# Two causal attention layers: heads in two 64-row strips, the triangle zeroed after the exponential, the key mask as a contraction row

## The chip, the cores and the metric

The kernel runs on one core of a Trainium2 chip. The metric is device time in microseconds (us), here the median of three runs. An instruction's line (L460 is line 460 of the kernel before) names where it is written; matmuls of the attention layers all go through one helper, so they carry L460 (matmul) or L463 (transpose) and are told apart by their tiles.

The engines: PE multiplies matrices (PEld are its weight loads), DVE is the vector engine, ACT the scalar engine, POOL is GpSimd, and SP is the sync engine, which here only issues DMAs. A "q" behind a name (SPq, ACTq) is that engine's sequencer, where DMA issues are shown.

## The reference

A pre-norm decoder with four blocks of self-attention, cross-attention and a feed-forward layer: 8 batches, 256 positions, 128 channels, 512 context positions, all float32. Only two of the twelve layers are changed, both in the last block. Both are causal with 16 heads of 8 channels:

```python
# L3_attn
scores = jnp.einsum('bhid,bhjd->bhij', Qh, Kh) / jnp.sqrt(jnp.asarray(Dh, dtype=x.dtype))
causal = jnp.tril(jnp.ones((S, S), dtype=x.dtype))
scores = scores * causal - NEG_BIG * (1.0 - causal)
attn = jax.nn.softmax(scores, axis=-1)
# L3_xattn: keys from the context
scores = jnp.where(mask[:, None, None, :] == 0, neg_inf, scores)
future = jnp.triu(jnp.ones((Sq, Sk), dtype=bool), k=1)
scores = jnp.where(future[None, None, :, :], neg_inf, scores)
attn = jnp.nan_to_num(jax.nn.softmax(scores, axis=-1), nan=0.0)
```

In L3_xattn the triangle hides every key past 255, so only the first 256 context positions take part. Its output is multiplied by a sigmoid gate of the queries before the output projection.

## The kernel before

`_heads_attention` (L478) computes five attention layers with many heads, the two causal ones with `causal=True`. Everything stays in SBUF. One **step** of its loop (the `while t < end` near L690) is one head of one batch: 16 heads times 8 batches make 128 steps, with a software pipeline:

- `maxima(t)`: the scores of head t with queries on the partitions, in two matmuls (`mh_sps`, 128x128 and 128x256, because the upper right quarter is not needed). DVE takes the row maxima off them in one custom reduce each (L523), which also adds the causal mask (a bf16 tile, `causal`; in L3_xattn a tile `km_q` that holds the key mask too).
- `turn`, every four heads: POOL splits the negated maxima into a rounded part and a rest (`mh_hi`, `mh_nx`; L549, L551, L552).
- `turned`, two steps later: PE transposes them (`mh_mps`, L463), ACT copies them to `mh_m` (L561), and a DMA on ACT's queue (L563) writes them into rows 96 and 97 of the query tile `mh_q`, so that the next matmul subtracts them.
- `exps(t-12)`: the scores again, keys on the partitions (`mh_bsps`): first a bf16 matmul that writes the mask (the identity times the triangle, 256 columns, in L3_attn; `km_k` times the identity, 384 columns, in L3_xattn), then two matmuls of 256 and 128 columns onto it. ACT takes the exponential (L583, `mh_e`).
- `combine`, every four heads, 16 steps behind `maxima`: 16 matmuls `mh_ops` that multiply by the values; four heads sit on four 32-column strips of the array. Then copies (`mh_osb`, L629), transposes (`mh_otps`), the division, and once per batch the output projection (`mh_yps`), the residual and the next layer's normalization.

While batch b runs, `hd.steps(b + 1)` prepares the next one: at head 2 the keys are projected (`mh_kps`, biased on ACT at L426, split in two parts on POOL at L428 and L429 into `mh_kp`), at head 3 the queries (`mh_qps`), and at heads 5 to 10 SP's queue spreads them over partitions: 4 DMAs of 16x8x256 for keys (L434) and 8 of 8x8x256 for queries (L439) into `mh_k` and `mh_q`. A head's 8 channels, in hi and lo parts, take 32 rows; even heads lie in rows 0 to 31 and odd ones in 32 to 63 of a 96-row contraction with zeros between. There are two key tiles of two halves, two query tiles, and a third query tile that `third()` (L377) sets up with four ACT copies and, for the key mask, the transposed triangle `causal_t` on POOL, between the layers at 1284 us.

The key mask is prepared by `_l3_masks` (L792) at step 72 of L3_attn: a 1 MB load that repeats the mask on all partitions, four DVE operations (L804), and then `key_bias`, for each batch two `km_q` (L813, L814) and two `km_k` operations on POOL (L816, L817).

PE's order is that of the program. The order on the other engines is set by the scheduler of the language, among what each pool's buffers allow: `mh_sps` and `mh_ops` share three PSUM buffers, `mh_bsps` has three, everything else two (`hd_g`). While L3_attn starts, the last normalizations of the layer before run as a "guest", at the pace given; the normalization of the following layer's input is part of this loop.

Of the kernel before, what the change touches and what calls it, by code (L numbers as in the profile page):

```python
# [40 lines left out]
P = 128  # L41
# [5 lines left out]
TOP = 96  # L47
FLOOR = -1.0e20
# [118 lines left out]
def _pack(inputs):  # L167
# [3 lines left out]
    for layer, mats in w.items():  # L171
# [8 lines left out]
    arrays["key_mask"] = np.ascontiguousarray(np.asarray(inputs["mask_BxS2_ik0"])[:, :S]).reshape(1, B * S)  # L180
    arrays["key_mask_t"] = np.ascontiguousarray(
        np.asarray(inputs["mask_BxS2_ik0"])[:, :S].reshape(B, 2, P).transpose(2, 0, 1)
    ).reshape(P, 2 * B)
# [161 lines left out]
class _Heads:  # L345
# [5 lines left out]
    def __init__(self, E, ctx):  # L351
# [10 lines left out]
        self.made = 0  # L362
# [14 lines left out]
    def third(self, ctx):  # L377

        pool = ctx.enter_context(self.E.tc.tile_pool(name="hd3", bufs=1, side="right"))
        q = pool.tile([P, H, S], F32R, name="mh_q2")  # L380
        for i in range(0, H, 4):
            self.E.nc.scalar.copy(
                q[:, i : i + 4, :].rearrange("p h n -> p (h n)"), self.E.plain[:, 0:1].to_broadcast([P, 4 * S])
            )
        self.q.insert(0, q)

        t = self.E.causal_t = pool.tile([P, 3, P], F32, name="causal_t")
        self.E.nc.gpsimd.memset(t, 0.0)
        for i in (0, 2):
            self.E.nc.gpsimd.affine_select(  # L390
                out=t[:, i, :], in_=t[:, i, :], compare_op=ALU.is_ge, fill=NEG, base=0,
                pattern=[[1, P]], channel_multiplier=-1,
            )

    def begin(self, layer, keys, bias=True):

        E, nc, W = self.E, self.E.nc, self.E.w(layer)
        self.layer, self.keys, self.bias = layer, keys, bias
        self.n = keys(0).shape[1]
        self.ready = {}  # L400
        if bias:

            ps = self.g.tile([P, D], F32, tag="g", name="mh_bps")
            bvt = self.one.tile([P, D], F32, tag="bvt", name="mh_bvt")
            nc.gpsimd.tensor_copy(bvt, W("bv").to_broadcast([P, D]))
            nc.tensor.matmul(ps, bvt, W("wo"), start=True, stop=True)
            self.row = self.one.tile([P, D], F32, tag="row", name="mh_row")
            nc.vector.tensor_tensor(self.row, ps, W("bo"), ALU.add)

    def steps(self, b):  # L410
# [29 lines left out]

        def values():
# [11 lines left out]
        two = lambda f, g: lambda: (f(), g())  # L453
        spread = [lambda j=j: spread_k(j) for j in range(4)]
        spread += [lambda r=r, j=j: spread_q(r, j) for j in range(4) for r in range(2)]
        early = [lambda: project("k", self.keys(b), n), lambda: project("q", E.xt(b), S), rest]
        return early, [two(*spread[i : i + 2]) for i in range(0, 12, 2)], values
# [20 lines left out]
def _heads_attention(E, ctx, causal=False, mask=None, key_bias=None, gate=False, guest=None, known=(0,), pace=None):  # L478
# [10 lines left out]
    lag = 12 if causal else 8  # L489
# [4 lines left out]
    pe = pool("mhe", 8 if causal else 10)  # L494
# [13 lines left out]
    units, extras = {}, {}  # L508

    def maxima(t):  # L510

        b, h = divmod(t, H)
        if h == 0 and key_bias:
            extras[b] = key_bias(b)
        if h % 4 == 0:
            u = units[t // 4] = SimpleNamespace(r=ready[b], es={}, extra=extras.get(b))
            u.nm = sm.tile([P, 2, 4], F32, name="mh_nm")
        u = units[t // 4]
        q, k = u.r.q[:TOP, h, :], u.r.k[:TOP, h // 2, :]
        def lowest(at, scores, lowered):  # L520

            rest = wk.tile([P, S if causal else n], BF16, name="mh_rest")
            nc.vector.tensor_tensor_reduce(  # L523
                rest[:, : scores.shape[1]], scores, lowered, -1.0, -FLOOR, ALU.add, ALU.min, accum_out=at
            )

        col = slice(h % 4, h % 4 + 1)
        if causal:
            ps = ps_a.tile([P, 3 * P], F32, tag="a", name="mh_sps")
            mm(ps[:, :P], q[:, :P], k[:, :P], start=True, stop=True, skip_group_check=True)  # L530
            mm(ps[:, P:], q[:, P:], k, start=True, stop=True, skip_group_check=True)
            by = (u.extra or E.causal)[0].rearrange("p i k -> p (i k)")
            lowest(u.nm[:, 0, col], ps[:, :P], by[:, :P])
            lowest(u.nm[:, 1, col], ps[:, P:], by[:, P:])
            return
        for c in range(2):
            ps = ps_a.tile([P, n], F32, tag="a", name="mh_sps")
            mm(ps, q[:, c * P : c * P + P], k, start=True, stop=True, skip_group_check=True)
# [5 lines left out]
    def turn(i):  # L544

        u = units[i]
        nm = u.nm
        hi = sm.tile([P, 2, 4], F32R, name="mh_hi")
        nc.gpsimd.tensor_copy(hi, nm)  # L549
        u.nx = sm.tile([P, 2, 2, 4], F32, name="mh_nx")  # L550
        nc.gpsimd.tensor_copy(u.nx[:, :, 0, :], hi)  # L551
        nc.gpsimd.tensor_tensor(u.nx[:, :, 1, :], nm, hi, ALU.subtract)  # L552

    def turned(i):
# [3 lines left out]
        for c in range(2):  # L558
            turn_over(ps[:8, c, :], u.nx[:, c, :, :].rearrange("p a h -> p (a h)"))
        m = wk.tile([8, S], F32R, name="mh_m")  # L560
        nc.scalar.copy(m, ps[:8].rearrange("p c q -> p (c q)"))  # L561
        h0 = 4 * (i % 4)
        nc.scalar.dma_start(u.r.q[TOP : TOP + 2, h0 : h0 + 4, :].bitcast(F32), m.bitcast(F32))  # L563

    def exps(t):

        u, h = units[t // 4], t % H
        if causal:
            ps = ps_b.tile([P, 384], F32, tag="b", name="mh_bsps")
            if u.extra:  # L570
                mm(ps, E.ident16, u.extra[1], start=True, stop=False, skip_group_check=True)
            else:
                mm(
                    ps.rearrange("p (i q) -> p i q", q=P)[:, 0:3:2, :], E.later,
                    E.ident16.unsqueeze(1).to_broadcast([P, 2, P]), start=True, stop=False, skip_group_check=True,
                )
            for kt in range(2):
                mm(
                    ps[:, 256 * kt : 256 + P * kt], u.r.k[:, h // 2, kt * P : kt * P + P],
                    u.r.q[:, h, kt * P :], start=False, stop=kt == 1, skip_group_check=True,  # L580
                )
            e = pe.tile([P, 384], F32, tag="e", name="mh_e")
            nc.scalar.activation(e, ps, AF.Exp, scale=scale)  # L583
            u.es[h % 4, 0], u.es[h % 4, 1] = e[:, :S], e[:, S:]
# [48 lines left out]
    def divide(b, s2):  # L633
# [8 lines left out]
        if key_bias is not None:  # L642
# [34 lines left out]

    normed_already = set(range(B) if guest is None else known)
# [10 lines left out]
    free = lag + 4  # L689
    t, end = 0, H * B + lag + 4  # L690
    while t < end or todo:
# [18 lines left out]
        if t < H * B:  # L710
            maxima(t)
            if t % 4 == 3:
                turn(t // 4)
        if guest:
            visit(pace(t))
        if t % 4 == 1 and 4 < t < H * B + 2:
            turned(t // 4 - 1)
        if 0 <= t - lag < H * B:
            exps(t - lag)
        c = t - lag - 4  # L720
# [71 lines left out]
def _l3_masks(E, ctx):  # L792
# [3 lines left out]
    mk = ctx.enter_context(E.tc.tile_pool(name="kmb", bufs=2))  # L796
    kb = pool.tile([P, B, 2, P], BF16, name="km")
    kt = pool.tile([P, B, 2], F32, name="km_t")
    with E.tc.tile_pool(name="km_raw", bufs=1) as rp:
        raw = rp.tile([P, B * S], I32, name="km_raw")  # L800
        nc.sync.dma_start(raw, E.ins["key_mask"].to_broadcast([P, B * S]))
        flat = kb.rearrange("p b i k -> p (b i k)")
        for i in range(0, B * S, 512):
            nc.vector.tensor_scalar(flat[:, i : i + 512], raw[:, i : i + 512], 0.0, NEG, ALU.is_equal, ALU.mult)  # L804
        rt = rp.tile([P, B * 2], I32, name="km_rt")
        nc.sync.dma_start(rt, E.ins["key_mask_t"])
# [975 lines left out]
```

## Time and profile before

| what | us |
| --- | --- |
| median of 3 runs (lowest, highest) | 1773.42 (1773.2, 1773.54) |
| span of the profiled execution | 1770.2 |
| L3_attn, first key projection to that of the next layer | 1325.7 to 1527.8 |
| L3_xattn, first key projection to its end | 1527.8 to 1707 |
| PE busy in the whole span | 1462.7 (83%) |
| DVE, ACT, POOL busy | 1148.5, 881.5, 495.7 |

The profiled execution's own time is not listed beside these runs; its span is 3.2 us below the median. Busy time is the time in which an engine has at least one instruction running, and matmuls overlap, so a busy PE can still be given more work; where PE's cost is at stake, the distance from one start to the next is read. A row of the timeline view gives the start, the duration, engine, line, operation, output and inputs, the number of instructions and, in brackets, how long the engine had been idle and what released it. The row of a DMA issue gives the time that the issuing engine spends on it, not the transfer's. A figure in the PEclk column is the clock that the throttle granted to PE, as a share of full speed.

### The profile page before, as it was taken

The page shows a single profiled execution, that of the slowest core. Times are in us where ns is not written, and L with a number is a line of the kernel's source. Part 1 is how long each engine was busy: PE and PEld are TensorE (multiplying, and loading weights), DVE is VectorE, ACT ScalarE, POOL GpSimd, SP SyncE. Part 2 cuts the span into 40 slices and gives each one's busy share as a digit, 9 for nine tenths or more (in the row PEclk, how much of TensorE's full clock was granted, in tenths as well). Part 3 has the DMA queues.
Part 4 walks back from the last instruction along what each step waited for, and adds up shares of the span by engine and source line. Part 5 has one row for each costly group of instructions (what it writes and reads, how often), then busy time and mean ns, then how long its engine had stood idle before and what let it go on. Part 6 is the DMA issues. An engine that isn't in the chain of part 4 may idle for free. (4 is left out here: it accounts for less than half of the span.)

```text
span 1770.2 us, 29308 instructions
## 1 busy us (share of the span) xinstructions
PE 1462.7 (83%) x10103; PEld 1055.3 (60%) x10141; DVE 1148.5 (65%) x3857; ACT 881.5 (50%) x1830; POOL 495.7 (28%) x987
## 2 busy tenths in 40 slices
PE   5689989999999998785578888878946799799986
PEld 3457677766665555453446666656615677677763
DVE  4567666765636676777667777767465666466756
ACT  7245455555652344325535655557644466355543
POOL 3122222221110122223433433332113433244422
PEclk9799999999999999997979999989956899899998
DMA  4011011104100000000111101111002221122100
GB/s 154 13 37 36 6 34 37 36 11 155 38 1 1 1 1 1 0 1 1 36 35 36 28 14 37 37 37 45 2 10 65 85 69 38 50 55 59 39 1 25
DMA packets 47236, 60.43 MB, mean 34 GB/s; under 512 B 5232, under 2 KB 36976, under 8 KB 46448
## 3 DMA queue, kind: packets, MB, share of 16 engines
q1 hardware_dynamic: 44720, 56.99, 11.9%
q8 instruction: 80, 1.31, 0.3%
q10 hardware_dynamic: 2368, 1.57, 0.3%
q14 instruction: 68, 0.56, 0.1%
HBM read 14.50 MB, written 1.05 MB: 9 GB/s over the span
## 5 line engine op out<-in xcount | busy, mean ns | idle before, releaser
L460 PE MATMUL mh_sps<-mh_k,mh_q 96*128 96x512 f32 (+2 forms) x1024 | 323.4, 398 | 49.0 <-DMA mh_q<-mh_qp 16.9
L460 PE MATMUL mh_bsps<-mh_q,mh_k 128*128 128x256 f32 (+1 forms) x1536 | 352.7, 335 | 7.6 <-ACT mh_e L596 4.1
L596 ACT ACTIVATE mh_e<-mh_bsps 128x512 f32<-128x512 f32 x512 | 281.0, 599 | 117.6 <-PE mh_bsps L460 110.4
L460 PEld LDWEIGHTS mh_bsps<-mh_q,mh_k 128*128 128x128 f32 x1536 | 265.8, 198 | 32.6 <-issue 6.9
L460 PEld LDWEIGHTS mh_sps<-mh_k,mh_q 96*128 96x128 f32 x1024 | 172.5, 202 | 96.2 <-issue 35.9
L523 DVE CUSTOM_DVE_ANT_0 mh_rest<-mh_sps,mask_b 128x512 bf16<-128x512 f32 x256 | 167.2, 685 | 81.4 <-PE mh_sps L460 78.4
L460 PE MATMUL mh_ops<-mh_e,mh_v 128*32 128x256 f32 (+1 forms) x3072 | 194.0, 373 | 1.3 <-DVE mh_nm L523 0.8
L542 DVE TENSOR_REDUCE mh_nm<-mh_sps 128x1 f32<-128x512 f32 x256 | 165.0, 680 | 25.7 <-PE mh_sps L460 25.2
L583 ACT ACTIVATE mh_e<-mh_bsps 128x384 f32<-128x384 f32 x256 | 118.6, 494 | 57.8 <-PE mh_bsps L460 33.5
L460 PEld LDWEIGHTS mh_ops<-mh_e,mh_v 128*32 128x32 f32 x3072 | 94.5, 111 | 66.1 <-ACT mh_e L583 5.8
L197 POOL TENSOR_SCALAR ln_rstd<-ln_mv 128x2 f32<-128x2 f32 x96 | 22.0, 229 | 386.4 <-DVE ln_mv L195 386.1
L549 POOL CAST mh_hi<-mh_nm 128x8 fp32r<-128x8 f32 x128 | 25.0, 195 | 337.9 <-DVE mh_nm L523 211.4
L523 DVE CUSTOM_DVE_ANT_0 mh_rest<-mh_sps,causal 128x128 bf16<-128x128 f32 (+1 forms) x256 | 79.4, 352 | 51.0 <-PE mh_sps L460 49.0
L523 DVE CUSTOM_DVE_ANT_0 mh_rest<-mh_sps,km_q 128x128 bf16<-128x128 f32 (+1 forms) x256 | 79.4, 350 | 43.8 <-PE mh_sps L460 42.5
L561 ACT CAST mh_m<-mh_mps 8x256 fp32r<-8x256 f32 x128 | 46.2, 361 | 102.1 <-PE mh_mps L463 100.2
L215 ACT COPY xt<-ln_ps 128x256 f32<-128x256 f32 x96 | 36.0, 375 | 120.5 <-PE ln_ps L463 62.3
L629 ACT COPY mh_osb<-mh_ops 128x256 f32<-128x256 f32 x128 | 47.7, 372 | 83.5 <-PE mh_ops L460 83.3
L886 ACT ACTIVATE moe_si<-moe_gps 128x512 f32<-128x512 f32 x64 | 38.0, 597 | 102.5 <-PE moe_gps L884 87.6
L460 PE MATMUL mh_bsps<-mask_t,ident 128*128 128x512 bf16 x219 | 84.7, 387 | 0.4 <-ACT mh_e L596 0.4
L201 DVE TENSOR_SCALAR ln_z<-x,ln_mv,ln_rstd 128x128 f32<-128x128 f32 x136 | 43.4, 360 | 54.9 <-POOL ln_rstd L198 54.7
L884 PE MATMUL moe_ups<-xt,w_L_ffn 128*128 128x512 f32 x128 | 69.2, 623 | 6.9 <-ACT moe_si L886 4.8
L463 PE MATMUL mh_mps<-ident,mh_nx 128*8 128x128 f32 x256 | 51.1, 282 | 27.7 <-POOL mh_nx L552 23.2
(360 smaller groups left out, 3086.8 us busy)
## 6 DMA issues: line engine op xcount, KB each, us to landing
mh_k<-mh_kp SPq DMA_DIRECT2D x64, 256.0 KB
mh_q<-mh_qp SPq DMA_DIRECT2D x256, 64.0 KB
mh_k<-mh_kp SPq DMA_DIRECT2D x64, 128.0 KB
w_L_ffn<-in_w_L_ffn SPq DMA_DIRECT2D x2, 1558.0 KB
w_L_attn<-in_w_L_attn SPq DMA_DIRECT2D x2, 1056.0 KB
ctx_t<-in_ctx_t SPq DMA_DIRECT2D x4, 512.0 KB
mh_q<-mh_m ACTq DMA_DIRECT2D x128, 8.0 KB
w_L_ffn<-in_w_L_ffn SPq DMA_DIRECT2D x2, 687.0 KB
```

The lines of the kernel that those rows point to most:

```text
L201: (engine or nc.vector).tensor_scalar(z[:, q, :], E.x[:, 2 * b + q, :], mv[:, q, 0:1], rstd[:, q : q + 1], ALU.subtract, ALU.mult)
L215: E.nc.scalar.copy(E.xt(b), ps.rearrange("p q t -> p (q t)"))
L460: return self.E.tc.keep_in_program_order(self.E.nc.tensor.matmul(*a, **kw))
L463: return self.E.tc.keep_in_program_order(self.E.nc.tensor.transpose(*a))
L523: nc.vector.tensor_tensor_reduce(rest[:, : scores.shape[1]], scores, lowered, -1.0, -FLOOR, ALU.add, ALU.min, accum_out=at)
L542: nc.vector.tensor_reduce(u.nm[:, c, col], ps, AX.X, ALU.max, negate=True)
L561: nc.scalar.copy(m, ps[:8].rearrange("p c q -> p (c q)"))
L583: nc.scalar.activation(e, ps, AF.Exp, scale=scale)
L596: nc.scalar.activation(e, ps, AF.Exp, scale=scale)
L629: nc.scalar.copy(osbs[b][:, u4 % 2, :], ops)
L884: nc.tensor.matmul(ps, W("w13")[:, o : o + P], xt, start=True, stop=True)
L886: nc.scalar.activation(si, pgate, AF.Silu)
```

## The change

Only the causal layers are changed, in these parts:

- **Strips.** Heads alternate between rows 0 to 63 and 64 to 127 of the array: head h lies in strip h % 2, slot h // 2. A maxima matmul contracts 33 rows (32 of the head, one for the key mask), the transposed one 35 (two more for the maxima). The two query tiles become four halves; the third tile and `causal_t` go. `strips()` writes the constant rows with 12 DMAs on SP's queue, once, when L3_attn begins.
- **Interleaving.** The lag of `exps` goes from 12 to 13 steps, so that it works on the other strip than `maxima`, and `by_turns` interleaves their four matmuls. `combine` comes 19 steps after `maxima`, not 16, and `turned` one step later; the pool of `mh_e` has 10 buffers, not 8.
- **Masks.** The mask matmul goes. The triangle is set to zero after the exponential, on POOL, one affine select of 128x2x128 per head. The key mask becomes a row of the contraction: `_l3_masks` is now a load of 8 rows and one DVE operation, and two small DMAs per batch copy a row of it to the key tile (`lower_k`). `key_bias` and its tiles go. DVE's reduce takes the plain causal tile in both layers.
- **Transfers.** Keys are spread by 8 DMAs of 8x8x256 per batch, not 4. The maxima of four heads are written by two DMAs, one per strip, and issued by SP, not by ACT.

The order of SP's queue in the changed program, per batch of L3_attn: one of the key spreads, the two maxima transfers of the previous batch's last four heads, seven key spreads, two maxima transfers, eight query spreads, and two more pairs of maxima transfers. In L3_xattn the maxima pair and the first `lower_k` come before the key spreads and the second `lower_k` after them. The core of the diff:

```diff
-    lag = 12 if causal else 8
+    lag = 13 if causal else 8
...
         if causal:
+            rows = slice(STRIP * (h % 2), STRIP * (h % 2) + EXTRA + 1)
+            q, k = u.r.q[rows, h // 2, :], u.r.k[rows, h // 2, :]
             ps = ps_a.tile([P, 3 * P], F32, tag="a", name="mh_sps")
-            mm(ps[:, :P], q[:, :P], k[:, :P], start=True, stop=True, skip_group_check=True)
-            mm(ps[:, P:], q[:, P:], k, start=True, stop=True, skip_group_check=True)
-            by = (u.extra or E.causal)[0].rearrange("p i k -> p (i k)")
+            yield mm(ps[:, :P], q[:, :P], k[:, :P], **go)
+            mm(ps[:, P:], q[:, P:], k, **go)
+            by = E.causal.rearrange("p i k -> p (i k)")
...
         nc.scalar.copy(m, ps[:8].rearrange("p c q -> p (c q)"))
+        if causal:
+            for r in range(2):
+                at = STRIP * r + EXTRA + 1
+                to = u.r.q[at : at + 2, 2 * (i % 4) : 2 * (i % 4) + 2, :]
+                nc.sync.dma_start(to.bitcast(F32), m[4 * r : 4 * r + 4, :].bitcast(F32))
+            return
...
         if causal:
-            ps = ps_b.tile([P, 384], F32, tag="b", name="mh_bsps")
-            if u.extra:
-                mm(ps, E.ident16, u.extra[1], start=True, stop=False, skip_group_check=True)
-            else:
-                mm(
-                    ps.rearrange("p (i q) -> p i q", q=P)[:, 0:3:2, :], E.later,
-                    E.ident16.unsqueeze(1).to_broadcast([P, 2, P]), start=True, stop=False, skip_group_check=True,
-                )
+            rows = slice(STRIP * (h % 2), STRIP * (h % 2) + EXTRA + 3)
+            q, k = u.r.q[rows, h // 2, :], u.r.k[rows, h // 2, :]
+            ps = ps_b.tile([P, 3 * P], F32, tag="b", name="mh_bsps")
             for kt in range(2):
-                mm(
-                    ps[:, 256 * kt : 256 + P * kt], u.r.k[:, h // 2, kt * P : kt * P + P],
-                    u.r.q[:, h, kt * P :], start=False, stop=kt == 1, skip_group_check=True,
-                )
-            e = pe.tile([P, 384], F32, tag="e", name="mh_e")
-            nc.scalar.activation(e, ps, AF.Exp, scale=scale)
+                yield mm(ps[:, 256 * kt : 256 + P * kt], k[:, kt * P : kt * P + P], q[:, kt * P :], **go)
+            e = pe.tile([P, 3, P], F32, tag="e", name="mh_e")
+            flat = e.rearrange("p i q -> p (i q)")
+            nc.scalar.activation(flat, ps, AF.Exp, scale=scale)
+            own = e[:, 0:3:2, :]
+            nc.gpsimd.affine_select(
+                out=own, in_=own, compare_op=ALU.is_ge, fill=0.0, base=0, pattern=[[0, 2], [1, P]],
+                channel_multiplier=-1,
+            )
...
+    def by_turns(s, e):
+
+        left = object()
+        while left is not None:
+            left = next(s, None)
+            left = next(e, None) or left
...
-        if t < H * B:
-            maxima(t)
-            if t % 4 == 3:
-                turn(t // 4)
+        s = maxima(t) if t < H * B else iter(())
+        e = exps(t - lag) if 0 <= t - lag < H * B else iter(())
+        if causal:
+            by_turns(s, e)
+        else:
+            _run(s)
+        if t < H * B and t % 4 == 3:
+            turn(t // 4)
...
-        if t % 4 == 1 and 4 < t < H * B + 2:
+        if t % 4 == (2 if causal else 1) and 4 < t < H * B + 3:
             turned(t // 4 - 1)
-        if 0 <= t - lag < H * B:
-            exps(t - lag)
-        c = t - lag - 4
+        _run(e)
+        c = t - lag - 4 - 2 * causal
...
+        ks = [lambda r=r, j=j: strip(k, "k", (0, 1, 0, 1), r, j) for j in range(4) for r in range(2)]
+        qs = [lambda r=r, j=j: strip(q, "q", (0, 0, 1, 1), r, j) for j in range(4) for r in range(2)]
+        if self.key_bias is not None:
+            ks.append(lower_k)
+        parts = [all_of(ks[:4]), all_of(ks[4:])] + [all_of(qs[i : i + 2]) for i in range(0, 8, 2)]
```

## The prediction

> **What bounds the kernel now.** The page gives a span of 1770.2 us; the median run took 1773.42, so 3.2 us lie outside the span and I take them as unchanged. Only two of the twelve layers change, and by the first PE instructions of their batches they fill 1325.7 to 1527.8 (L3_attn) and 1527.8 to 1707 (L3_xattn). I first read busy time by stretches of 20 us (columns: us, then busy us and instructions of PE, weight loads, DVE, ACT, POOL, then granted clock, DMA share, GB/s):
>
> ```profile
> 1380.00:1400.00 20.00, 14.13 (x129) 11.51 (x128) 13.10 (x66) 8.75 (x21) 13.21 (x26) 0.91 0.34 102
> 1400.00:1420.00 20.00, 16.45 (x135) 13.50 (x136) 9.57 (x59) 10.22 (x25) 5.71 (x19) 0.83 0.29 90
> 1440.00:1460.00 20.00, 18.73 (x186) 15.59 (x185) 12.63 (x82) 12.14 (x30) 6.83 (x20) 1.00 0.23 64
> 1600.00:1620.00 20.00, 18.75 (x180) 15.63 (x178) 12.82 (x73) 12.20 (x30) 9.54 (x22) 1.00 0.18 51
> ```
>
> In steady state PE is busy 18.7 of 20 us at full clock and no other engine passes 13: PE bounds both layers. The first mh_kps matmul of each batch gives the period: in L3_attn 22.5, 20.8, 32.5, 19.2, 19.3, 19.2 us, in L3_xattn 19.8 and then 21.1. The 32.5 is the first two rows. What PE, then POOL did in it:
>
> ```profile
> 1392.80 0.59 PE L463 MATMUL mh_mps<-ident,mh_nx 128*8 128x128 f32 x2 [3.12 <-POOL mh_nx L552]
> ...
> 1402.99 0.59 PE L463 MATMUL mh_mps<-ident,mh_nx 128*8 128x128 f32 x2 [4.19 <-POOL mh_nx L552]
> ```
>
> ```profile
> 1386.64 0.78 POOL L813 TENSOR_TENSOR km_q<-causal,km 128x256 bf16<-128x256 bf16 x1 [1.63 <-DVE km L804]
> ...
> 1391.34 1.10 POOL L816 TENSOR_SCALAR km_k<-causal_t,km_t 128x256 bf16<-128x256 f32 x1
> 1392.40 0.18 POOL L551 COPY mh_nx<-mh_hi 128x8 f32<-128x8 f32 x1
> ```
>
> The reader is to see PE waiting for the maxima that POOL splits, and POOL late because eight key-mask operations (two batches) queue ahead of and between them; after each wait the granted clock falls, so a wait is paid twice. In the steady part one head pair on PE looks like this:
>
> ```profile
> 1451.28 0.44 PE L460 MATMUL mh_sps<-mh_k,mh_q 96*128 96x128 f32 x2
> 1451.56 0.28 PE L460 MATMUL mh_bsps<-ident,causal 128*128 128x256 bf16 x1
> 1451.60 0.43 PE L460 MATMUL mh_bsps<-mh_q,mh_k 128*128 128x256 f32 x2
> 1451.96 0.90 PE L460 MATMUL mh_ops<-mh_e,mh_v 128*32 128x256 f32 x16
> 1452.79 0.50 PE L460 MATMUL mh_sps<-mh_k,mh_q 96*128 96x128 f32 x2
> ```
>
> From the mask matmul at 1450.98 to the next at 1451.56 is 0.58 us: one head in L3_attn; in L3_xattn, where the mask is 384 wide, 0.62 to 0.65. Durations overlap, so I count starts. Last, SyncE's queue:
>
> ```profile
> 1612.02 2.65 SPq L434 DMA_DIRECT2D mh_k<-mh_kp  x4
> 1614.78 10.29 SPq L439 DMA_DIRECT2D mh_q<-mh_qp  x8
> 1633.15 2.67 SPq L434 DMA_DIRECT2D mh_k<-mh_kp  x4
> ```
>
> Four issues back to back take 2.67 us, 0.67 each, whatever they carry; they land 2.2 to 2.4 us after their issue begins. Twelve a batch (8 us) are no bound today.
>
> **The change, part by part.**
>
> *Mask matmuls go; heads alternate in strips (PE).* 128 matmuls of 256 columns (L3_attn) and 128 of 384 (L3_xattn) with their loads disappear. By starts a mask costs about 0.09 to 0.13 in L3_attn, so the other four matmuls of a head are 0.45 to 0.54 one after the other. If two strips run side by side they shrink towards half, 0.27. No row in the trace has two row strips, so this is unknown; the nearest row is the 16 mh_ops matmuls, on four strips of 32 columns: three of 256 columns start within 14 ns (1451.957, 1451.964, 1451.971), where the full-height matmuls follow each other at 0.11 to 0.2. But the same place shows a price for changing the array's split: 0.15 us from the last mh_bsps to the first mh_ops load, 0.20 from the last mh_ops to the next load. About 13 of 16 steps of a batch have other work (mh_mps, mh_ops, mh_otps, projections, mh_yps) between strip matmuls, so I charge about 0.2 us a head. Ends: 0.27 (overlap, no price) to 0.74 (none, full price). I take 0.28+0.2 = 0.48 by the mh_ops row, so PE's batch becomes 19.2−16×0.10 = 17.6 or less in L3_attn and 21.1−16×0.15 = 18.7 in L3_xattn. PE stops being the only bound.
>
> The Trainium skill, "TensorEngine Tiling (Array Packing)", section Key Properties, says both: different tiles load and multiply in parallel, and changing the tiling mode drains the array. The second speaks against a kernel that switches up to 26 times a batch. The same page (Gotcha 1: PSUM Pressure) wants different row tiles on different PSUM banks; the two score tiles come from different pools. By the first rule alone PE's head would be 0.27; with the second it is what I take. No run so far shows row tiles.
>
> *Maxima transfers move from ACT's queue to SP's (two per four heads).* ACT loses 4×0.62 = 2.5 us a batch of blocked sequencer; it is not the bound (12.2 of 20), worth nothing by itself. SP now issues 8 k + 8 q + 8 maxima = 24 a batch, and 26 in L3_xattn with the key-bias rows: 24×0.67 = 16.1 us, 26×0.67 = 17.4. SP runs in order. From mh_kps to the first k issue is 2.27 us (1609.75 to 1612.02). In the changed program's order for L3_attn, one k issue is followed by two maxima, seven k, two maxima (the batch's first four heads) and eight q: the last q starts 19×0.67 = 12.7 after the first k and lands 2.2 later, so the next batch's q is there 17.2 us after mh_kps. Its first head stands 14 steps after mh_kps, and the next mh_kps two steps (about 1.0 each when nothing waits) after that: the loop closes at about 19.2 us. The second unit's maxima wait behind all eight q: issued at about +15.7, landed at +18, needed 15 steps after mh_kps. So the period is about 19.2 (L3_attn) and, with two more issues a batch, 19.5 (L3_xattn). **This is what is late next.** Ends per batch: −2.2 (queue not binding, PE's 17) and +1.3 (an issue waiting for a maxima copy with q behind it). Against 19.2 and 21.1 that gives 0 and −1.6. The Trainium skill, "DMA: Bandwidth & Descriptors", section Issuing engines are not separate DMA queues, says that spreading issues over engines saves only sequencer time; here that time is the very thing that runs out.
>
> *Triangle zeroed on POOL.* 16 affine selects a batch on 128x2x128 f32. The trace has it only as 128x128: 292 ns (L390, twice). Ends: 0.29 and, from the 128x256 TENSOR_SCALAR of L816, 0.95; I take 0.40, the 128x256 POOL cast at L428 (0.40). 16×0.40 = 6.4 a batch. POOL goes from 6.8 to 13.2 (L3_attn), and from 10.2 − 2.65 + 6.4 = 14 (L3_xattn, where the four key-mask operations a batch, 0.67+0.43+0.95+0.60, go): hidden beside PE while under 19. The deciding size is (19.2−6.8)/16 = 0.78. It adds a link exp→select→mh_ops; combine is two steps later (2.4 us), which covers it. Behind it on POOL wait mh_hi/mh_nx: up to a few 0.4s, and turned is a step later (1.2 us).
>
> *Key mask as a row.* The 1 MB load, 2.44 us of DVE (L804, four pieces) and the eight POOL operations before 1395 (5.7 us) go; a load of 8 rows and one DVE operation come. The 32.5 period becomes about 23 to 25 (the norm work of the following layer stays): −8. Ends −4 and −11.
>
> *Starts and ends.* First fill of L3_attn: PE already waits 9.31 us for mh_q (1338.36); four more k issues: +2.7, I take +2. The 12 strip-filling DMAs lie in the layer before (1284 to 1325, 12×0.67 = 8 us of SP): hidden; without cover +8, so kept in the range. third()'s four ACT copies there (about 1 us each) save at most that. The last batch of each layer has no k/q behind it and runs at PE's pace: −2 and −3. Longer pipeline (lag +1, combine +2 steps): +1.5 at each drain.
>
> *Sum:* stall −8; L3_attn steady 0; fill +2; its last batch −2, drain +1.5; L3_xattn six periods ×−1.6 = −9.6; last batch −3; drain +1.5. Total −17.6 → 1773.4−17.6 = **1756**.
>
> **Rivals.**
> 1. *The queue does not bind* (the loop has slack, or PE halves truly): periods 17 and 17.5. Seven L3_attn periods ×−2.2 = −15, eight L3_xattn ×−3.6 = −29, stall −8, fill and drains +5: −47 → **1726**. For: the 0.015 us starts of mh_ops. Against: 16 us of SP issues in a 17 us period.
> 2. *Slower: strips do not overlap*, and switching still costs 0.2: 0.69 a head against 0.58 and 0.63: +0.11×16×8 = +14, +0.06×16×8 = +8, stall −8, fill and drains +5: +19 → **1792**. Decides where a head passes about 0.59 in L3_attn. For: every step brings other work between the strips. Against: the mh_ops row.
> 3. *Slower: POOL becomes the bound*: at 0.95 a select POOL has 22 and 22.8 us a batch: +2.8×7 and +1.7×7, −8, +5: +28 → **1801**. Decides at 0.78 us.
> 4. *Even:* the SP queue stalls once per batch on a maxima copy, 20.5 a period: +1.3×7 and +1×7 on the forecast → **1772**.
>
> **How the numbers follow.** About 0.2% (3.5 us) is what a measurement of this kernel can tell from no change. Chances: forecast 0.40 (its own range 1744 to 1768), rival 1 0.23, rival 4 0.05, rival 2 0.21, rival 3 0.11. Faster 0.63, same 0.05, slower 0.32. The range reaches from 1722 to 1796, taking in rivals 1 and 2 and the key-mask ends; what lies outside is most of rival 3 and the edges of rivals 1 and 2.
>
> **What would show it.** Right: mh_kps starts 19 to 19.5 apart in both layers, SP issues back to back, PE busy under 17 of 20, waits of mh_sps or mh_bsps for DMA into mh_q; no period over 26. Wrong: strip matmuls of opposite strips starting over 0.1 apart in pairs with no gain per head (rival 2); selects over 0.78 or PE waiting for mh_nx in most batches (rival 3); periods of 17 with gaps on SP (rival 1). The forecast also fails if PE waits let the clock fall in steady state, as at 1400 to 1420 (0.83): that alone is worth 17% of a batch.

## The result, and the profile after

The changed kernel takes **1836.72 us** (median of 5 runs, 1823.01 to 1837.82) where the kernel before took 1773.54 in the same sitting: 1.0339 times as long, 95% interval 1.0309 to 1.037. The forecast was 1756 with a range to 1796; none of its rivals gives 1837. The profiled execution is the fastest of the five, with a span of 1821.3 us, so what it shows is the milder form. In the experiments below medians are of all executions, while ratios and intervals leave out those that fell in a slower state (one of four in e1 and in e8, three of four in e4).

First the busy times by stretches of 20 us of the changed kernel (columns as before; granted clock third from the end):

```profile
1380.00:1400.00 20.00, 19.51 (x128) 12.08 (x126) 11.81 (x65) 10.32 (x24) 10.67 (x29) 0.50 0.13 37
1400.00:1420.00 20.00, 19.36 (x123) 11.59 (x122) 11.03 (x67) 9.35 (x22) 11.78 (x30) 0.50 0.15 40
1440.00:1460.00 20.00, 19.93 (x160) 11.95 (x160) 12.93 (x82) 11.62 (x29) 10.93 (x30) 0.69 0.23 68
1600.00:1620.00 20.00, 16.72 (x163) 10.38 (x162) 13.25 (x78) 12.13 (x30) 12.86 (x36) 0.93 0.21 56
```

The rows of before had a clock of 1.00 in the steady part. In the first two rows here PE is busy nearly all the time and the clock is 0.50. The first mh_kps matmuls of the batches stand 23.5, 26.1, 29.3, 25.8, 20.4 and 19.6 us apart in L3_attn, and in L3_xattn 24.6 and 26.7 where the clock is low and 20.9, 20.2, 20.0 where it is mostly up. Between 1340 and 1700 the clock is low for 261 us, in the kernel before for 42.

What the heads look like on PE, at full clock and then at half (same kernel, same view). Two `mh_sps` rows and two `mh_bsps` rows are one head's share of a step; the row behind them is other work:

```profile
1655.91 0.32 PE L487 MATMUL mh_sps<-mh_k,mh_q 33*128 33x128 f32 x1
1655.91 0.38 PE L487 MATMUL mh_bsps<-mh_q,mh_k 35*128 35x256 f32 x1
1656.07 0.33 PE L487 MATMUL mh_sps<-mh_k,mh_q 33*128 33x256 f32 x1
1656.13 0.22 PE L487 MATMUL mh_bsps<-mh_q,mh_k 35*128 35x128 f32 x1
1656.33 0.86 PE L487 MATMUL mh_ops<-mh_e,mh_v 128*32 128x256 f32 x16
```

```profile
1415.85 0.47 PE L487 MATMUL mh_sps<-mh_k,mh_q 33*128 33x128 f32 x1
1415.86 0.58 PE L487 MATMUL mh_bsps<-mh_q,mh_k 35*128 35x256 f32 x1
1416.13 0.52 PE L487 MATMUL mh_sps<-mh_k,mh_q 33*128 33x256 f32 x1
1416.23 0.30 PE L487 MATMUL mh_bsps<-mh_q,mh_k 35*128 35x128 f32 x1
1416.58 0.59 PE L490 MATMUL mh_mps<-ident,mh_nx 128*8 128x128 f32 x2
```

The strips do run side by side: two matmuls of opposite strips start in the same hundredth of a microsecond, and a head with the pause behind it takes 0.42 us (1655.91 to 1656.33), less than the 0.48 forecast. At half clock the same head takes 0.73 (1415.85 to 1416.58). So the step that I doubted most holds, and the clock takes back more than it gives.

What PE waits for in the stretch where the clock is mostly up, 1600 to 1660 (us in total, times, longest us; line numbers are those of the kernel shown):

```profile
PE mh_sps L487 <- DMA mh_q<-mh_m: 4.3, 3, 2.2
PE mh_sps L487 <- DMA mh_q<-mh_qp: 1.8, 2, 1.6
```

These are waits of about 2 us per batch for transfers on SP's queue, of the kind that the forecast named. Three of them stand in this stretch, and the clock falls after each. After those that end at 1618.62 and 1638.76 (2.19 and 1.93 us) it is low for 3.41 us, one record. After the third it is low for 27 times as long, from 1660.6 to 1752.7:

```profile
1658.83 0.29 PE L487 MATMUL mh_sps<-mh_k,mh_q 33*128 33x128 f32 x1 [1.64 <-DMA mh_q<-mh_qp]
```

In 1421 to 1447, at half clock, the same view lists no wait of PE at all, and no weight load there waits over 0.4 us for another engine. So waits can start a low clock here, but it stays low without them.

### The profile page after: what moved, and what is told of

Read it like the earlier page. It is cut to its first block, busy times and chain, and to the rows that moved or that the text cites. A ratio compares the mean times of both kernels' runs of the same rounds, so it can differ in the third digit from the quotient of the medians.

```text
span 1821.3 us, 29541 instructions
## 1 busy us (share of the span) xinstructions
PE 1522.8 (84%) x9847; PEld 1028.3 (56%) x9885; DVE 1149.2 (63%) x3856; ACT 884.3 (49%) x1826; POOL 574.0 (32%) x1208
## 4 chain that ended last, share of the span: by engine, by line
PE 57%; DVE 21%; POOL 9%; ACT 5%; issue 4%; DMA 2%; SPq 1%; ACTq 0%; POOLq 0%; DVEq 0%
PE mh_sps L487 9%; PE mh_ops L487 9%; PE mh_bsps L487 9%; DVE mh_nm L570 3%; PE moe_dps L921 2%; POOL ln_rstd L196 2%; PE mh_otps L490 2%; PE mh_mps L490 2%; DVE mh_rest L541 2%; PE moe_gps L910 2%; PE moe_ups L910 2%; PE fa_kvps L487 2%; PE la_cps L487 2%; PE mh_kps L487 2%; POOL fa_v L1163 1%
## 5 line engine op out<-in xcount | busy, mean ns | idle before, releaser
L487 PE MATMUL mh_sps<-mh_k,mh_q 96*128 96x512 f32 (+2 forms) x1024 | 354.7, 447 | 55.7 <-DMA mh_q<-mh_qp 21.2
L487 PE MATMUL mh_bsps<-mh_q,mh_k 128*128 128x256 f32 (+2 forms) x1536 | 375.6, 359 | 13.0 <-DMA mh_q<-mh_m 8.9
L487 PEld LDWEIGHTS mh_bsps<-mh_q,mh_k 128*128 128x128 f32 (+1 forms) x1536 | 280.9, 220 | 41.4 <-issue 15.6
L487 PEld LDWEIGHTS mh_sps<-mh_k,mh_q 96*128 96x128 f32 (+1 forms) x1024 | 192.7, 235 | 161.0 <-issue 79.2
L541 DVE CUSTOM_DVE_ANT_0 mh_rest<-mh_sps,causal 128x128 bf16<-128x128 f32 (+1 forms) x512 | 159.0, 351 | 132.2 <-PE mh_sps L487 90.2
L487 PE MATMUL mh_ops<-mh_e,mh_v 128*32 128x256 f32 (+1 forms) x3072 | 211.2, 413 | 0.7 <-DVE mh_nm L570 0.3
L616 POOL TENSOR_SCALAR_AFFINE_SELECT mh_e<-mh_e 128x256 f32<-128x256 f32 x256 | 103.6, 413 | 124.3 <-ACT mh_e L614 123.4
L921 PEld LDWEIGHTS moe_dps<-w_L_ffn,moe_act 128*128 128x128 f32 x512 | 64.7, 200 | 15.7 <-issue 8.7
```

Source lines behind the costliest of these rows:

```text
L487: return self.E.tc.keep_in_program_order(self.E.nc.tensor.matmul(*a, **kw))
L541: nc.vector.tensor_tensor_reduce(rest[:, : scores.shape[1]], scores, lowered, -1.0, -FLOOR, ALU.add, ALU.min, accum_out=to)
L616: nc.gpsimd.affine_select(out=own, in_=own, compare_op=ALU.is_ge, fill=0.0, base=0, pattern=[[0, 2], [1, P]], channel_multiplier=-1,)
L921: nc.tensor.matmul(ps[:, t, :], act[:, c, t * P : t * P + P], W("w2")[:, o : o + P], start=c == 0, stop=c == 1)
```

## What the granted clock follows

The trace records the granted clock in stretches that are whole multiples of 3.41 us (but for the one that the end cuts off), at 0.5 or 1.0. I estimated, for each such window between 1340 and 1760 us, the array's work: over the matmuls that start in it, columns streamed, times rows contracted / 128, times columns of weights / 128 (in blocks of 32), over the cycles in the window. A score or bf16 matmul counts one cycle per column, other float32 ones two, since 128 columns follow each other at 0.108 and 0.213 us at half clock. Over thirteen traces (both kernels and e1 to e11 below), of the windows at half clock with work below 0.50, 2 of 245 were followed by full clock; of those above 0.70, 85 of 125. Between the two lie some 400 windows, the largest group, and about 30 of them were followed by full clock, so the estimate ranks windows and gives no sharp threshold. Full clock was lost after windows with a median of 0.22 and kept after windows with 0.53. In the changed kernel the windows that stayed at half (the staying windows below) have a median of 0.51, the nine that released it 0.71. Without the weight by rows the two medians are 0.81 and 0.84, which separates next to nothing. This was theory A's later form, and it is a correlation; the experiments with 65, 128 and 62 rows below test whether rows matter.

The Trainium skill, "TensorE: Matmul & The Clock Gate", section Part 1: The HAM clock gate, has the two clock states and a window of 3413 ns, which these records show too. It puts the release down to sustained activity and has idle gaps as what loses it. Here 26 us without a wait of PE were not released, so for strips the measurement says more: being busy without gaps was not enough, and the experiments below show that the number of rows at work matters.

## The experiments

**Theory A**: strips keep too little of the array at work, so the clock stays low. **Theory B**: PE's waits behind SP's queue pull the clock down. **Theory C**: POOL's select lengthens the step. The kernel before was run beside each; ratios are to it.

**e1_warm**: an idle full-array matmul per head.

```diff
+            yield mm(own, E.causal[:, 0, :], E.ident16.unsqueeze(1).to_broadcast([P, 2, P]),
+                start=True, stop=True, skip_group_check=True)
             for kt in range(2):
...
```

> The changed kernel with one matmul more per head: the old triangle matmul (bf16, 256 columns on the full array) is written into the score tile and at once overwritten by the real scores, so that it does nothing but keep the array at work. Theory A (the array is at work too little with strips, so the granted clock stays at half even where PE waits for nothing): the clock in L3_attn and L3_xattn goes from about 0.6 and 0.7 to over 0.9, the periods of a batch from 26 to 19.5 to 21, and the time to 1750 to 1785, although PE has 0.1 us more to do per head. Theory B (the clock falls because PE waits for transfers on SP's queue, and work added changes nothing in that): the clock stays where it is and the time is 1835 to 1860. Theory C (POOL's select makes the step longer): as B.

Measured: 1866.97 us, 1.0534 (1.0446 to 1.0622), low clock through most of L3_attn and the first part of L3_xattn (to 1659), periods of 30.8 at low clock in L3_attn. As A stood, this is a miss. The estimate above, worked out later, fits it: 256 columns are 0.21 us at half clock in a step of 1.9, which lifts the staying windows' median only from 0.51 to 0.54. The matmul adds 0.21 us of work and makes the step longer, by 0.31 us (periods of 30.8 against 25.8).

**e2_serial**: `by_turns(s, e)` becomes `_run(s)`, `_run(e)`.

> The changed kernel without the interleaving: the two maxima matmuls of a head, then the two transposed ones of the other head, so a strip follows itself and two strips overlap only at the seam. Theory A, if what counts is how many rows are at work at a time: the clock stays at half nearly everywhere, PE needs 0.1 to 0.2 us more per head, 1840 to 1880. Theory A, if what counts is only how long some matmul streams, whatever its rows: the clock rises over 0.9, 1760 to 1800. Theory B: about as the changed kernel, 1820 to 1850.

Measured: 1838.83, 1.0363 (1.0306 to 1.0421), as the changed kernel. PE streams for longer, one strip at a time, and the clock does not rise: this speaks against the form of A in which only the time that some matmul streams counts (1760 to 1800). It doesn't decide between the rest, since the time lies in B's range and just under that of A by rows.

**e3_fullrows**: every score matmul contracts 128 rows. The scores of two heads are then added up, and the exponential takes a thousandth of them, so the result is another one.

```diff
-            rows = slice(STRIP * (h % 2), STRIP * (h % 2) + EXTRA + 3)
+            rows = slice(0, P)
...
-            nc.scalar.activation(flat, ps, AF.Exp, scale=scale)
+            nc.scalar.activation(flat, ps, AF.Exp, scale=1e-3 * scale)
```

> The changed kernel with every score matmul contracting all 128 rows, so that the scores of two heads are added up (the exponential takes a thousandth of them, to stay finite): the same instructions, transfers, waits and POOL work, but no strips. Theory A: the clock is over 0.95, PE does a head in about 0.45 to 0.55 us, the period is about 19 to 20 and the time 1745 to 1775. Theory B and C: the clock stays as in the changed kernel or lower, since matmuls no longer overlap, 1830 to 1870.

Measured: 1768.51, 0.9986 (0.9972 to 1.0). The same transfers and POOL work, the same kind of waits, and 68 us less than the changed kernel. B and C fall as explanations of the slowdown. PE still waits for the maxima, here over 1560 to 1700:

```profile
PE mh_sps L487 <- DMA mh_q<-mh_m: 8.2, 5, 2.4
```

In L3_xattn's steady part each such wait costs one or two windows of low clock here and then it comes back; the changed kernel has low stretches of 35, 14 and 27 windows. The clock is not over 0.95, as A had it: between 1340 and 1700 it is low for 97 us, more than in the kernel before and far less than in the changed one. Two stretches:

```profile
1400.00:1420.00 20.00, 18.74 (x164) 15.33 (x164) 13.39 (x87) 12.26 (x30) 12.90 (x36) 0.84 0.37 117
1440.00:1460.00 20.00, 16.64 (x160) 14.01 (x159) 11.58 (x74) 11.75 (x29) 12.47 (x37) 0.91 0.21 57
```

**e4_maskmm**: strips, the old mask matmul instead of the select.

```diff
+            yield mm(own, E.causal[:, 0, :], ..., start=True, stop=False, skip_group_check=True)
...
-            nc.gpsimd.affine_select(
```

> The changed kernel with the triangle added by the old bf16 matmul of 256 columns ahead of each head, in both layers, and no select on POOL. Theory A: as the kernel with the idle matmul, within 8 us, 1745 to 1785, clock over 0.9. Theory C: the select is the cost, so this is well below the kernel with the idle matmul (by over 15 us). Theory B: 1825 to 1860.

Measured: 1827.32, but single runs from 1778.64 (mean clock 0.91) to 1866.47 (0.858). Inconclusive on C: four times spread over 88 us give no ratio. They rise as the mean clock falls, but why one kernel's clock differs so much between executions is not shown.

**e8_rows65**: as e3, with `rows = slice(0, STRIP + 1)`.

> The changed kernel with every score matmul contracting rows 0 to 64 (65 rows: one head's strip and the first row of the other; the second strip's scores are left out, and the exponential takes a thousandth), so that the array is used at full height, without strips, overlap or changes of mode, but with 65 rows and not 128. If rows in use are what keeps the clock up, in blocks of 32: three quarters of the array, clock between the changed kernel's and that of the 128-row kernel, 1768 to 1800. If the changes of mode (the pauses between strips and the rest) keep it down: as the 128-row kernel, 1765 to 1775.

Measured: 1810.35 (single runs 1797.73 to 1827.84), 1.0191 (1.0132 to 1.025); low clock for 214 us between 1340 and 1700, against 97 in e3. It differs from e3 in one thing, 65 rows instead of 128, and by the ratios costs some 36 us more. There are no strips in it and no changes between strips and the full height, so these are not needed to keep the clock down. The time is at the upper end of the range expected for blocks of 32 or over it.

**e12_rows62**: strips filled up with rows in which the key tile is zero.

```diff
-STRIP, EXTRA = 64, 32
+STRIP, EXTRA, LAST = 64, 32, 62
...
-            rows = slice(STRIP * (h % 2), STRIP * (h % 2) + EXTRA + 1)
+            rows = slice(STRIP * (h % 2), STRIP * (h % 2) + LAST)
...
-            rows = slice(STRIP * (h % 2), STRIP * (h % 2) + EXTRA + 3)
+            rows = slice(STRIP * (h % 2), STRIP * (h % 2) + STRIP)
```

> The changed kernel with the strips filled up: rows 33 to 61 of each strip of the key tile are zero (one-time copies), the maxima rows move to 62 and 63, and the score matmuls contract 62 and 64 rows instead of 33 and 35: same strips, same changes of mode, same overlap, same numbers out. If the clock is released by the rows of the array at work, counted one by one (the weight that tells released windows best in the traces so far), the work of a window at half clock rises from about 0.51 to 0.60 of the array, just into the range in which windows were released: the stretches of low clock get shorter, 1775 to 1815. If rows count in blocks of 32 (33 rows are two blocks already) or the changes of mode are what counts: no change, 1823 to 1840.

Measured: 1790.1, 1.0084 (1.0051 to 1.0116): 47 us less than the changed kernel, for rows of zeros. Between 1340 and 1700 the clock is low for 193 us, not 261. Of the windows at half clock between 1340 and 1760, 13 of 61 were followed by full clock, in the changed kernel 9 of 91. The staying windows' median is 0.57. The stretch after the key mask, and a later one:

```profile
1400.00:1420.00 20.00, 16.68 (x133) 10.39 (x131) 12.54 (x76) 9.86 (x25) 13.09 (x36) 0.75 0.23 60
1600.00:1620.00 20.00, 17.03 (x170) 10.80 (x165) 13.57 (x81) 12.22 (x30) 13.30 (x37) 0.91 0.21 56
```

33 and 62 rows are the same number of blocks of 32, and so are 35 and 64, so rows count in finer steps than blocks of 32; that they count one by one fits, but no run shows it. With this and e8 it is shown by intervention, not only by correlation, that the rows at work change how long the clock stays low. The exact weights of the estimate are not shown.

**e9_burst**: the changed kernel, 40 idle matmuls before L3_attn's first head.

```diff
+        for _ in range(40):
+            mm(ps, E.ident16, E.causal.rearrange("p i k -> p (i k)"), start=True, stop=True, skip_group_check=True)
```

> The changed kernel with 40 idle matmuls (bf16, 384 columns, full array, into a buffer that nobody reads) ahead of L3_attn's first head, where PE waits some 10 us for the first query transfers. Theory A in its present form (a low clock is released only by a window of 3.4 us with about 70% of the array's rows at work, which strips don't reach; a full clock falls only in a window with under about 40%): the first heads run at full clock, and it lasts until the first wait of 2 us or more; the stretch of low clock from 1333 to 1452 gets shorter by 20 to 100 us, each worth about a quarter of itself: 1805 to 1835 against some 1830. If the strips alone pull the clock down, whatever it was: no change, 1823 to 1845.

Measured: 1836.52, 1.0344 (1.0317 to 1.0371), no change and over A's range. The clock was up from 1331.9 to 1342.2, when the first head began after a wait of 4.42 us for its query transfer, and fell there; it then stayed low for 25 windows. Raising the clock once was worth nothing here, where the stream doesn't bring it back.

**e7_actq**: `nc.sync.dma_start` of the maxima becomes `nc.scalar.dma_start`.

> The changed kernel with the maxima transfers issued by ACT again (still two per four heads). Theory A: the transfers that PE waits for come earlier, so at full clock the periods fall from 20 to 17 to 19 and the clock falls less often, but where it is low it stays low, since the strips are unchanged: 1795 to 1830. Theory B (the waits are the whole cause): the clock is over 0.9 in both layers and the time 1735 to 1765.

Measured: 1902.18, 1.075 (1.0719 to 1.0781), a miss for both theories. Over 1420 to 1520 SP's query spreads wait:

```profile
SPq L449 <- DMA mh_q<-mh_m: 42.5, 15, 7.2
```

A query spread waits for ACT's transfers into the query tile. It did so in the kernel before too (17.5 us, 8 times, over 1420 to 1520), and in the changed kernel, where both are on SP, the view lists no such wait. PE then waits 19.2 us for the late spreads. So moving the maxima to SP, which I priced only as 5 us of issues, avoids a wait. That this wait is all of the 65 us, and that the split of the tiles into halves makes it longer, is argued from the traces and not isolated by a run.

**e13_fewer**: e3 with four of the eight key transfers left out, so that half of the key rows hold old values.

```diff
-        ks = [... for j in range(4) for r in range(2)]
+        ks = [... for j in range(2) for r in range(2)]
```

> The 128-row kernel (no strips, the clock mostly up, 1768.5) with four of the eight key transfers of a batch left out, so that half of the key rows hold old values: SP issues 20 and 22 a batch in place of 24 and 26. If SP's queue sets the period there (its issues stand nearly back to back, and PE waits 1 to 2 us a batch for transfers into mh_q), four issues of 0.67 us less take 2 to 2.7 us off each period: 17 to 18 us, the waits for mh_q and the one low-clock window after each of them go, time 1725 to 1748. If POOL or DVE set it: 1760 to 1772.

Measured: 1733.3, 0.9768 (0.9747 to 0.9789). Periods of 16.7 to 18.6, no wait for mh_q left in 1560 to 1680. SP's queue is what sets e3's 19 to 21, as the forecast had it, at 35 us for four issues a batch.

**e5_keyrow**: the kernel before, with only the key mask as a row (98 of 128).

```diff
...
+        def lower_k():
+            src = self.key_bias[b : b + 1, :]
+            nc.sync.dma_start(k[TOP + 2 : TOP + 3, :, :].bitcast(F32), src.unsqueeze(1).to_broadcast([1, H // 2, n]))
...
```

> The kernel before with only the key mask changed: a row of the contraction (row 98 of the 128 that the transposed scores contract anyway), no km tiles, no key-mask work on POOL, and the triangle alone as mask matmul (256 columns) in both layers; the maxima are taken without the key mask, which the row sums divide out. No strips, no select. Both theories expect a gain: the 32.5 us period becomes 22 to 26, L3_xattn's periods go from 21.1 to 19.5 to 20.5, time 1752 to 1766, clock as before (0.92 or more over the span). If the stall was worth nothing, 1770 to 1775.

Measured: 1768.63, 0.9984 (0.9974 to 0.9994). The period of 32.5 became 26.9 and L3_xattn's 21.1 became 20.4, and from the first mh_kps to the last the trace is 8.0 us shorter (318.3 for 326.3). It reaches the first mh_kps 2.7 us later than the kernel before, which is scatter: the traces here reach it anywhere from 1323.8 to 1331.8. The median gained only about 3 us, less than expected. Of the two waits for mh_nx in the long period one is left, with the key-mask operations gone:

```profile
1401.05 0.59 PE L466 MATMUL mh_mps<-ident,mh_nx 128*8 128x128 f32 x2 [5.15 <-POOL mh_nx L553]
```

In the 7 us before it POOL works on normalizations (`ln_rstd`, `ln_z`, `x`) and DVE waits for them, so the key mask was only a part of what made mh_nx late.

**e6_select** and **e10_select_long**: e5 with the triangle zeroed on POOL and no mask matmul; then with the changed kernel's lag of 13, combine 19 steps behind and 10 buffers.

```diff
-    lag = 12 if causal else 8
+    lag = 13 if causal else 8
...
-        c = t - lag - 4
+        c = t - lag - 4 - 2 * causal
```

> The same with the triangle zeroed by POOL after the exponential and no mask matmul: the select without strips, maxima still on ACT's queue. Theory A (array activity, weighed by rows, sets the clock): full-height matmuls keep the clock up, PE's head shrinks from 0.58 to about 0.47, so 1735 to 1758. Theory C (the select is in the way): slower than the kernel with the key row alone by 5 to 40 us.

> The kernel with key row and select, without strips, with the longer pipeline of the changed kernel: lag 13, combine 19 steps behind the maxima, 10 buffers for the exponentials. If the 60 us that the select cost there were the wait of mh_ops for it (16.7 us of PE in 100, periods of 24 to 25.5), they go and PE's shorter head shows: periods of 17 to 18.5, time 1735 to 1762, below both kernels. If POOL itself is the limit or the clock falls with the mask matmul gone: over 1790.

Measured: 1832.29, 1.0339 (1.0311 to 1.0367), and 1772.09, 0.9988 (0.9973 to 1.0002), both over the ranges that A and the longer pipeline would have given. In e6 the clock is up (1.00 in 1600 to 1620) and PE waits, over 1560 to 1680:

```profile
PE mh_ops L463 <- POOL mh_e L580: 14.1, 16, 1.3
```

In e10 that wait is gone, and PE waits 10.8 us for mh_nx instead. The longer pipeline (lag, combine and buffers together) is worth the 60 us; another wait took over.

**e11_long_burst**: e10 with the 40 idle matmuls.

> The same with the 40 idle matmuls ahead of L3_attn's first head. With full-height matmuls the clock comes back by itself within some 20 us (at 1358 in the kernel before), so the burst is worth at most half of that: 0 to 10 us less than without it.

Measured: 1775.06, 0.9996 (0.9983 to 1.0009), no gain.

**e14_flat_sp**, **e15_flat_sp_late**, **e16_flat_act_late**: e10 with the maxima on SP's queue; that with `turned` one step later; and the later step with the maxima on ACT's queue.

```diff
-        if t % 4 == 1 and 4 < t < H * B + 2:
+        if t % 4 == (2 if causal else 1) and 4 < t < H * B + 3:
```

> The kernel with key row, select and longer pipeline but no strips (1772), with the maxima transfers moved from ACT's queue to SP's, as one transfer per four heads: 16 or 17 issues a batch on SP (11 us), none on ACT, and the query spreads no longer wait for ACT's maxima transfers (26.9 us of SP's waits in 80 before). If SP's queue and these waits set its period of 19.6 to 20.4: 17 to 18.5, time 1730 to 1755, clock over 0.91, below both kernels. If POOL's late mh_nx sets it (PE waits 10.8 us for it in 120): 1762 to 1775.

> The same with the transpose of the maxima one step later, as in the changed kernel. If PE's wait for mh_nx (up to 1.4 us, once per four heads, with POOL's selects in between) is what is left: 5 to 20 us less than with the transpose at the old step; else the same within 4 us.

> The kernel of 1729.6 (no strips, key row, select, longer pipeline, maxima transposed one step later) with the maxima transfers back on ACT's queue, one per four heads. If the later step alone did it: 1727 to 1740. If moving the transfers to SP's queue was needed as well (query spreads on SP wait for ACT's maxima transfers, which now come a step later still): 1750 to 1780.

Measured: 1776.93, 1.0002 (0.9982 to 1.0022); **1729.61**, 0.9741 (0.9704 to 0.9778); 1732.93, 0.9768 (0.9737 to 0.98). PE's wait for the maxima over 1560 to 1680, in e14 and in e15:

```profile
PE mh_mps L466 <- POOL mh_nx L553: 20.7, 16, 1.7
```

```profile
PE mh_mps L466 <- POOL mh_nx L553: 3.7, 5, 0.7
```

The queue was not needed, the step was: with POOL's selects mh_nx comes up to 1.7 us late, and one step of slack covers most of it (over 1560 to 1640, where both kernels are in L3_xattn, 14.4 us of waits against 3.7). The 47 us between e14 and e15 are more than the 5 to 20 that I expected. e15 leaves nothing out, has no strips, and is 46 us faster than the kernel before.

## Why the prediction was wrong, point by point

- **The failed step** is the first of the change's parts, where PE's batch became 17.6 and 18.7 us: it took every start from rows at clock 1.00 and left the clock there. I weighed overlap against changes of mode for PE's time, and not what fewer rows do to the clock. The last sentence of the forecast named a falling clock as what would break it, but as a matter of waits, and gave it no chance. Shown in its place: the strips leave the clock at 0.50 for long stretches, where a head takes 0.73 us and an L3_attn batch 25.8. With 128 rows instead of the strips the same program takes 1768.5; the difference of 68 us is larger than the 41 us by which the time missed the range.
- **Strips overlap**: right, 0.42 us a head at full clock against 0.48. Rival 2 fell.
- **SP's queue is next**: right in mechanism (e13), a little short in size: 20.0 to 20.9 in L3_xattn at mostly full clock, where I had 19.5. That is rival 4's 20.5, to which I gave 0.05, and SP does wait for ACT's copy of the maxima there (10.6 us over 1600 to 1660, up to 4.3 at a time). I also left out that each wait of about 2 us costs PE a window or more of low clock.
- **The select**: one takes 409 ns (0.40 forecast, rival 3's 0.95 fell):

```profile
L616 POOL TENSOR_SCALAR_AFFINE_SELECT mh_e<-mh_e 128x256 f32<-128x256 f32 x47 | 18.5, 409 | 11.5 <-ACT mh_e L614 11.4
```

  That combine's two steps cover it was right and worth 60 us (e6, e10). What I passed over as "a few 0.4s" on mh_nx costs 47 us where `turned` is not moved (e14, e15); the changed kernel has moved it, so this is no part of its slowdown.
- **The key mask**: mis-sized. The period went to 26.9, not 23 to 25, since the wait behind the normalizations stayed (e5); I had put both waits down to the key mask. Alone it gave about 3 us of the median, where I had −8 for this stall.
- **The maxima transfers**: I counted issues only; the wait of the query spreads for ACT's transfers, which is long in e7, I did not see.

What stays open: whether POOL or PE's stream is the next bound of e15; what lets the clock come back after one window in one place of the changed kernel and after 27 in the next; and the exact rule of the clock, since the work is estimated from starts and counted for matmuls alone.

## What to carry to other kernels

Before PE work is made smaller by using less of the array, ask what holds the clock up: a stream that is dense in time but thin in rows stayed at half clock here for up to 35 windows, and one wait of 1.64 us was followed by 92 us of it. If the rows have to be few, rows of zeros count as work: with them the strips took 47 us less. And a step of slack in front of a consumer can decide whether cheaper work pays: the select in place of the mask matmul made the kernel slower or left it even (e6, e14) until the later combine and the later transpose of the maxima let it gain (e15), and none of that needs strips.

## What the runs showed of the hardware that was not expected

- How long the clock stays low goes with the rows contracted, in finer steps than blocks of 32, and zeros count: 33 and 35 rows take 1.034 times the kernel before, 62 and 64 rows 1.008, the strips otherwise alike; without strips 65 rows take 1.019 and 128 rows 0.999.
- Two clock regimes persist side by side in one program: 35 windows of 3.41 us at half clock, with PE busy 20.00 of 20 us (1420 to 1440), then full clock in the same loop. The same kind of wait, 1.6 to 2.2 us long, was followed by 1, 1 and 27 such windows with strips, and by one each with 128 rows (1600 to 1650).
- A change from strips to other work is cheap beside this: about 0.2 us at full clock between the last strip matmul's start and that of the next kind (1656.13 to 1656.33).
